# Attention's side products: keys from the query product's free columns, values and output for two groups of heads at once, inverse sums by transfers, diagonal masks off TensorE

## The chip, the cores and the metric

The kernel runs on one core of one Trainium2 chip. The metric is the device time of one execution in microseconds (us). TensorE, VectorE (DVE), ScalarE (ACT), GpSimd (POOL) and SyncE (SP, which here only issues transfers) each work through their instructions in order and wait for each other through semaphores.

## The reference

The input x is 8 sequences of 1024 tokens of 128 features. A layer of relative-position attention with 8 heads of 16 features is followed by a mixture of 8 experts of which each token uses two:

```python
xn = (inputs - mu) / jnp.sqrt(var + 1e-05) * ln_gamma + ln_beta
xh = xn.reshape(b, s, H, Dh)
q = xh @ Wq + bq;  k = xh @ Wk + bk;  v = xh @ Wv + bv
p = pe @ Wp                                   # pe: sine and cosine of the position
content = jnp.einsum('bqhd,bkhd->bhqk', q + u_bias, k)
pos_score = _rel_shift(jnp.einsum('bqhd,khd->bhqk', q + v_bias, p))
attn = softmax((content + pos_score) / sqrt(e))
x = x + jnp.einsum('bhqk,bkhd->bqhd', attn, v).reshape(b, s, e) @ Wo + bo
# then, on layernorm(x): router (two products, layer norm, gelu), softmax, top 2 of 8,
# and for each expert:  x1, x2 = split(h @ W1[e] + b1[e]);  y = (x1 * gelu(x2)) @ W2[e] + b2[e]
output = output + y * expert_mask[:, :, e]    # and x + output
```

The relative shift makes a query's score with keys up to its own position, with the key just after it, and with later keys come from different rows of the position product; the kernel has two tables of key operands for this ("own" and "upper"), and the one key after the query is treated apart, as a band.

## The kernel before, in words

**Tiling.** The eight heads are two groups g of four. Each head has 32 of the 128 partitions: 16 for content and 16 for position. So one score product with 32 rows gives content and position scores together. A block n is a sequence b, a group g and a half qc of the queries (512 of them); there are 32 blocks in the order (b, g, qc). A block has nine units, and the main loop runs over steps t, one unit a step. In each step three blocks' stages overlap:

- side A: scores of queries by keys for the block at t. `greatest` takes each query's row maximum: units "own" (L574, with a table of masks, `wide`), "oth" (the other half of the keys, L570) and one unit "dia" (the four 128x128 blocks on the diagonal). Before the change "dia" adds a mask with a TensorE product (L562) into the bank and reduces it from there (L568).
- side B, 11 steps later: the transposed scores with the shift by the row's maximum (`lower`, L580) and ScalarE's exponential into px (`power`, L587). Upper and lower parts are cut on GpSimd (L597).
- 13 steps later: `weigh`, the product of values and px (av, L631), accumulated over the nine units.

A step has two half-steps, two heads on side A and two on side B in each. Half 0 has the av products, half 1 has `lower`. Each half-step's scores take four of six banks of PSUM; the next half-step's reuse those that the exponentials and the maxima free. A seventh bank, one alone, serves all side products ("ms").

**Side products.** Everything else of attention is written as generators. `aside` is called at the end of each half-step, and takes from the live generators by due time; at most one step that uses the ms bank (`yield 0` asks for it) goes into a half-step, and in half 0 such a step is put off if it is not due. An integer yielded is a number of half-steps to wait. The generators are: `prepare` (layer norm and transpose to xT, once a sequence); `keys` (once per sequence and group: products pq L444 twice for each half of the tokens, multiplied with tables tb on VectorE, L446, and added on GpSimd to z; the content keys' product pk L454; then twelve transfers that place kl and z in shifted copies ku and zu); `values` (product pv L477, transposed to va); `band` (pd, pb L500, pbt L507); `beside` (pm L640 and the band's exponential eb); `close`. After side A's last unit, `shifts` combines the maxima on VectorE (L607 to L613), splits them in three bf16 parts, and TensorE transposes them (mt, L618).

**Closing a block (before).** One column of each head's values is one, so av also holds the sums of the weights. `close` adds av and eb to cx, transposes it to pn (L658), takes the reciprocal of the sums (rd, L660), spreads it on GpSimd (rx, L662), transposes back to pr (L667), multiplies, and projects: po (L673), added to xall (L675).

**Routes and experts.** When the last block of every second sequence is closed, a route is queued: router products, top two, ranks, and 32 indirect transfers a route from GpSimd that scatter the tokens to their experts' rows (xs, L864). These too run beside attention. After attention, 71 blocks of 256 rows pass through the experts (L1189, L1190, L1200), each with its own load of weights (wb).

What stands around the change in the main loop:

```python
if half == 0:
    w = now(t, LAG_W)
    if w:
        weigh(*w)
        if w[1] == NU - 1:
            cl = close(w[0])
            ...
elif ua and ua[1] == NU - 1:
    sh = shifts(ua[0])
    ...
aside(2 * t + half, half == 0)
```

Of the kernel before, what the change touches and what calls it, by code (L numbers as in the profile page):

```python
# [49 lines left out]
P = 128  # L50
NB, S, D = 8, 1024, 128
H, DH = 8, 16
HG = 4
# [19 lines left out]
KB = REG // BT  # L73
# [81 lines left out]
def kernel(ctx: ExitStack, tc: tile.TileContext, a: dict, out: bass.AP):  # L155
# [25 lines left out]
    rows_bc = keep.tile([P, DR + NE], F32, name="rows_bc")  # L181
# [10 lines left out]
    wo_p = [keep.tile([P, D], F32, name=f"wo_p{g}") for g in range(NG)]  # L192
# [4 lines left out]
    rk = ctx.enter_context(tc.tile_pool(name="rk", bufs=1))  # L197
    rk2 = ctx.enter_context(tc.tile_pool(name="rk2", bufs=2))
# [51 lines left out]
    with ExitStack() as at:  # L250
# [34 lines left out]
        wk_p = [acst.tile([P, HG, 32], F32, name=f"wk_p{g}") for g in range(NG)]  # L285
        wv_p = [acst.tile([P, HG, 32], F32, name=f"wv_p{g}") for g in range(NG)]
        wc = [acst.tile([P, 2, P], F32, name=f"wc{g}") for g in range(NG)]
        bias = [acst.tile([P, 4], F32, name=f"bias{g}") for g in range(NG)]

        with tc.tile_pool(name="setup", bufs=1) as sp:  # L290
# [15 lines left out]
            row = sp.tile([1, DR + NE], F32, name="row")  # L306
            nc.scalar.dma_start(row[:, 0:DR], a["br1"].rearrange("(o p) -> o p", o=1))
            nc.scalar.dma_start(row[:, DR:], a["br2"].rearrange("(o p) -> o p", o=1))
            for g in range(NG):
                nc.vector.memset(wo_p[g], 0.0)  # L310
                for j in range(HG):
                    h = HG * g + j
                    nc.scalar.dma_start(wo_p[g][32 * j:32 * j + DH, :], a["Wo"][DH * h:DH * h + DH, :])
                nc.scalar.dma_start(kus[g], a["tab_u"][g])
            nc.scalar.dma_start(wo_p[0][DH:DH + 1, :], a["bo"].rearrange("(o p) -> o p", o=1))
# [21 lines left out]
            nc.tensor.matmul(pb[:, 0:DR + NE], lhsT=ones[0:1, :], rhs=row, start=True, stop=True)  # L337
            nc.vector.tensor_copy(rows_bc, pb[:, 0:DR + NE])
# [9 lines left out]
            wq_p = [sp.tile([P, HG, 32], F32, name=f"wq_p{g}") for g in range(NG)]  # L348
            for g in range(NG):
                for i, t in ((0, wq_p[g]), (1, wk_p[g]), (2, wv_p[g])):  # L350
                    nc.vector.memset(t, 0.0)
                    blocks(t[:, :, 0:DH], i, HG * g, HG)
# [10 lines left out]
            for g in range(NG):  # L363
# [9 lines left out]
                nc.vector.tensor_tensor(wc[g][:, 0, :], wc[g][:, 0, :], wq_p[g].rearrange("p j c -> p (j c)"), ALU.add)  # L373
# [5 lines left out]
                nc.tensor.matmul(pc[:, 2:4], lhsT=ppad, rhs=rp[:, 65:67], start=True, stop=True)  # L379
                nc.vector.tensor_copy(bias[g], pc[:, 0:4])  # L380
                nc.vector.tensor_tensor(bias[g][:, 3:4], bias[g][:, 3:4], cst[:, C_ONE:C_ONE + 1], ALU.add)
# [13 lines left out]
        def prepare(b):  # L395
# [17 lines left out]
            yield  # L413
            xts[b] = xt = ap1.tile([P, S], F32, name=f"xT{b}", tag="xT")
# [8 lines left out]
        def keys(b, g, s):  # L423
# [14 lines left out]
            for hf in range(NQ):  # L438
                c, tb = slice(hf * QB, hf * QB + QB), tbs[hf]
                ts = []  # L440
                for k in range(2):
# [3 lines left out]
                    t = ap1.tile([P, QB], F32, name=f"t{k}{u}_{hf}", tag=f"t{k}")  # L445
                    nc.vector.scalar_tensor_tensor(t, pq, bs[:, k:k + 1], tb[:, k, :], ALU.add, ALU.mult)  # L446
                    ts.append(t)
                    if k == 0:
                        yield
                nc.gpsimd.tensor_tensor(z[:, c], ts[0], ts[1], ALU.add)  # L450
                yield
                yield 0
                pk = bank(f"pk{u}_{hf}")
                nc.tensor.matmul(pk, lhsT=flat(wk_p[g]), rhs=xt[:, c], start=True, stop=True)  # L454
                nc.scalar.activation(kl[:, c], pk, AF.Identity, bias=bs[:, 2:3])
# [11 lines left out]
        def values(b, g, s):  # L467

            u, xt = f"{b}_{g}", xts[b]
            s["vt"] = vt = ap2.tile([P, S + 1], F32, name=f"vt{u}", tag="vt")  # L470
            s["va"] = va = ap2.tile([P, NT, P], F32, name=f"va{u}", tag="va")
            nc.vector.memset(vt[:, S:S + 1], 0.0)
            for hf in range(NQ):
                c = slice(hf * QB, hf * QB + QB)
                yield 0
                pv = bank(f"pv{u}_{hf}")
                nc.tensor.matmul(pv, lhsT=flat(wv_p[g]), rhs=xt[:, c], start=True, stop=True)  # L477
# [861 lines left out]
```

## Time and profile before

| | |
|---|---|
| median of 3 runs | 2161.19 us (2159.23 to 2165.55) |
| profiled execution | 2203.32 us, span 2201.6 us, mean granted TensorE clock 0.952 |
| first scores | at 65.0 us |
| attention | to about 1716 us |
| experts | from about 1724 us |
| TensorE, ScalarE, VectorE, GpSimd busy | 1958.0, 951.4, 1370.8, 742.1 us |
| exponentials px, L587 | 1152 of 594 ns |
| maxima oth, L570, and own, L574 | 512 of 685 ns, 512 of 688 ns |
| maxima dia, L568 | 128 of 686 ns |
| products pq, L444 | 75.0 us in all |

The profile is of one execution, which took longer than the runs that were timed; sums from it are held against its own time. In a line of a group, "x" is the number of instructions and the time behind it the mean of one. A product of 32-bit numbers appears as two instructions. A wait is put down to the instruction that came last, and "issue" is time for which the profile shows no cause. In the chain of what ended last, each row is its start, its length and the work that was waited for.

### The profile page before, as it was taken

To read this page: it belongs to the slowest core of one execution; us is meant where nothing else is said; L and a number is where in the kernel's file an instruction comes from. 1 tells how busy PE (TensorE), PEld (TensorE's weight loads), DVE (VectorE), ACT (ScalarE), POOL (GpSimd) and SP (SyncE) were. 2 spreads that over 40 slices of the span, in tenths; PEclk is the share of its full clock that TensorE was granted. 3 is DMA by queue.
4 is the path that set the end of the run, shared out by engine and by line. 5 is a ranking of instruction groups with operands and counts; after the bars stand their busy time and mean duration, and the time that the engine had idled before them with its cause. 6 is when DMAs were issued, how large, how long until landed. Compare 5 with 4: busy or idle time off the path is not lost.

```text
span 2201.6 us, 40140 instructions
## 1 busy us (share of the span) xinstructions
PE 1958.0 (89%) x15115; PEld 1059.7 (48%) x15115; DVE 1370.8 (62%) x3652; ACT 951.4 (43%) x1767; POOL 742.1 (34%) x895
## 2 busy tenths in 40 slices
PE   4899999999999999889998988998976898799995
PEld 2334444344443444334444433443432687678884
DVE  3476687777777668656876776676651355344454
ACT  0035545455554544445454534454442343234442
POOL 2021223213323331643134254324244244543353
PEclk9999999999999999899999998999996899899998
DMA  5101101101010110201010102010000445455596
GB/s 139 43 14 32 44 1 44 42 4 44 1 44 11 35 36 9 67 17 44 2 44 2 44 28 56 2 44 15 1 18 23 143 156 180 139 173 185 190 304 185
DMA packets 84983, 143.53 MB, mean 65 GB/s; under 512 B 12405, under 2 KB 55558, under 8 KB 84790
## 3 DMA queue, kind: packets, MB, share of 16 engines
q1 hardware_dynamic: 58480, 113.37, 17.8%
q0 software_dynamic: 8912, 18.15, 2.3%
q10 hardware_dynamic: 17398, 9.46, 1.6%
q8 instruction: 119, 1.95, 0.4%
q14 instruction: 74, 0.61, 0.1%
HBM read 105.06 MB, written 23.28 MB: 58 GB/s over the span
## 4 chain that ended last, share of the span: by engine, by line
PE 73%; DVE 11%; POOL 5%; issue 4%; ACT 3%; DMA 2%; another core or an unknown queue 1%; SPq 0%; ACTq 0%; POOLq 0%; DVEq 0%
PE sc L549 27%; PE av L631 10%; PE h L1189 6%; PE h L1190 6%; PE y L1200 5%; DVE jk L574 4%; PE pq L444 3%; PE sc L580 3%; ACT px L587 2%; PE sc L562 2%; PE pb L500 2%; POOL xs L864 2%; PE pk L454 1%; PE pv L477 1%; PE po L673 1%
## 5 line engine op out<-in xcount | busy, mean ns | idle before, releaser
L587 ACT ACTIVATE px<-sc 128x512 f32<-128x512 f32 x1152 | 624.1, 594 | 650.3 <-PE sc L549 310.6
L570 DVE TENSOR_REDUCE oth<-sc 128x1 f32<-128x512 f32 x512 | 330.1, 685 | 209.2 <-PE sc L549 154.9
L549 PE MATMUL sc<-kl,z 32*128 32x512 f32 (+3 forms) x1536 | 411.8, 566 | 44.0 <-ACT px L587 33.1
L574 DVE CUSTOM_DVE_ANT_0 jk<-sc,wide 128x512 f32<-128x512 f32 x512 | 352.2, 688 | 136.4 <-PE sc L549 93.1
L549 PE MATMUL sc<-ku,zu 32*128 32x128 f32 (+3 forms) x2304 | 377.5, 411 | 12.1 <-issue 5.3
L549 PE MATMUL sc<-zu,ku 32*128 32x512 f32 (+3 forms) x1536 | 369.2, 559 | 0.0
L549 PE MATMUL sc<-z,kl 32*128 32x512 f32 (+3 forms) x1536 | 340.9, 525 | 0.0
L631 PE MATMUL av<-px,va 128*32 128x512 f32 (+3 forms) x3072 | 319.3, 512 | 20.7 <-POOL px L597 20.7
L1193 DVE SCALAR_TENSOR_TENSOR gt<-h,wb,gl 128x256 f32<-128x256 f32 x284 | 137.2, 484 | 174.2 <-ACT gl L1192 147.9
L549 PEld LDWEIGHTS sc<-ku,zu 32*128 32x128 f32 x2304 | 196.1, 193 | 64.9 <-ACT px L587 38.5
L549 PEld LDWEIGHTS sc<-kl,z 32*128 32x128 f32 x1536 | 141.3, 191 | 162.8 <-ACT px L587 119.0
L1218 POOL DMA_INDIRECT ys<-yo,to x142 | 137.0, 965 | 236.9 <-DVE to L1214 102.4
L1192 ACT ACTIVATE gl<-h,wb 128x256 f32<-128x256 f32 x284 | 134.0, 473 | 170.7 <-PE h L1190 131.1
L1189 PE MATMUL h<-xt,wb 128*128 128x256 f32 x568 | 177.6, 395 | 32.4 <-ACT yb L1202 15.4
L597 POOL TENSOR_SCALAR_AFFINE_SELECT px<-px 128x516 f32<-128x516 f32 (+1 forms) x128 | 85.7, 669 | 358.2 <-ACT px L587 358.1
L1190 PE MATMUL h<-xt,wb 128*128 128x256 f32 x568 | 174.6, 390 | 0.0
L549 PEld LDWEIGHTS sc<-zu,ku 32*128 32x128 f32 x1536 | 120.7, 191 | 89.7 <-ACT px L587 66.4
L631 PEld LDWEIGHTS av<-px,va 128*32 128x32 f32 x3072 | 70.7, 111 | 187.1 <-issue 118.8
L549 PEld LDWEIGHTS sc<-z,kl 32*128 32x128 f32 x1536 | 129.8, 192 | 61.5 <-ACT px L587 27.7
L580 PE MATMUL sc<-mT,onesb 32*128 32x512 bf16 x1152 | 143.4, 388 | 9.0 <-ACT px L587 9.0
L864 POOL DMA_INDIRECT xs<-rw,slot x128 | 123.9, 968 | 37.3 <-issue 34.0
L1200 PE MATMUL y<-gt,wb 128*128 128x256 f32 x568 | 134.6, 380 | 0.3 <-ACT yb L1202 0.3
(287 smaller groups left out, 2457.1 us busy)
## 6 DMA issues: line engine op xcount, KB each, us to landing
wb<-in_wx SPq DMA_DIRECT2D x71, 772.5 KB
tb<-in_tab SPq DMA_DIRECT2D x32, 768.0 KB
xb<-xs SPq DMA_DIRECT2D x71, 130.0 KB
zu<-z SPq DMA_DIRECT2D x128, 64.0 KB
yk<-ys SPq DMA_DIRECT2D x32, 256.0 KB
ku<-kl SPq DMA_DIRECT2D x64, 64.0 KB
out<-yk ACTq DMA_DIRECT2D x16, 256.0 KB
xall<-in_inputs ACTq DMA_DIRECT2D x7, 512.0 KB
```

The costliest lines, as they stand in the source:

```text
L549: nc.tensor.matmul(ps[:, c0:c0 + w], lhsT=lhs[r, l0:l0 + P], rhs=rhs[r, r0:r0 + w], start=first, stop=final)
L570: nc.vector.tensor_reduce(oth[:, t, j:j + 1], p, AX.X, ALU.max)
L574: nc.vector.tensor_tensor_reduce(jk, p, wide[:, m0:m0 + QB], 1.0, 3.0 * BIG, ALU.add, ALU.max, own[:, t, j:j + 1])
L580: nc.tensor.matmul(p, lhsT=onesb[r, :], rhs=mts[n][r, :], start=first, stop=not first)
L587: nc.scalar.activation(pxs[n, k][:, j, :], p, AF.Exp)
L631: nc.tensor.matmul(avs[n][32 * j:32 * j + 32, c0:c1], lhsT=va[:, kt, 32 * j:32 * j + 32], rhs=px[:, j, c0:c1], start=(k == 0), stop=(k == ...
L864: return nc.gpsimd.indirect_dma_start(xs_v[2 * (t0 + n) + k], bass.IndirectOffsetOnAxis(ap=slot[:, n, k:k + 1], axis=0), rw[:, n, :], None)
L1189: nc.tensor.matmul(ph[:, 1, :], lhsT=wb[:, FF + c * P:FF + (c + 1) * P], rhs=xt, start=True, stop=True)
L1190: nc.tensor.matmul(ph[:, 0, :], lhsT=wb[:, c * P:(c + 1) * P], rhs=xt, start=True, stop=True)
L1193: nc.vector.scalar_tensor_tensor(gt[:, c, :], ph[:, 0, :], wb[:, B1_0 + c:B1_0 + c + 1], gl, ALU.add, ALU.mult)
L1200: nc.tensor.matmul(y, lhsT=wb[:, W2_0 + c * D:W2_0 + (c + 1) * D], rhs=gt[:, c, :], start=(c == 0), stop=(c == NFC - 1))
L1218: ins = nc.gpsimd.indirect_dma_start(ys_v[HB * i + k], bass.IndirectOffsetOnAxis(ap=to[:, k:k + 1], axis=0), yo[:, k, :], None).ins
```

## The change

- Keys: the product of the normalized tokens with `wc[g][:, 1, :]` has 16 columns per head which only position needed. The content keys' weights are added in its other columns, and kl is read from that bank (with a scale of 0 or 1 for each partition) before the product is used up; pk is gone.
- Values: `values` runs once a sequence. Both groups' values are in one product, and va holds for each head group 0's values, a column block of ones, and group 1's values; a group's 32 columns are taken from the middle outward. In group 1 the sums therefore come first. `beside` needs a row of ones in place of the other group's values, which one more GpSimd operation (v1) makes.
- Inverse sums: `close` sends the sums of cx through four transfers to 128 partitions (sm), takes the reciprocal, writes it to memory (inv) and reads it back spread over 16 partitions a head (rx); GpSimd multiplies. The wait between the steps is 3, 3 and 2 half-steps.
- Output: group 0's cx is kept; group 1's is added to it on GpSimd, and one product po with both groups' weights is made for two blocks. The output's bias is added to xall on GpSimd in `prepare`.
- Masks: a "dia" unit's scores are copied to SBUF by ScalarE (up), masked by GpSimd, and reduced by VectorE two half-steps later (`diagonal`).
- Order: `shifts` continues one half-step later. Some buffers change size or share a place, and beside the experts a step that asks for a longer wait gets it.

```diff
         def keys(b, g, s):
...
                     pq = bank(f"pq{u}_{hf}_{k}")
                     nc.tensor.matmul(pq, lhsT=wc[g][:, k, :], rhs=xt[:, c], start=True, stop=True)
-                    t = ap1.tile([P, QB], F32, name=f"t{k}{u}_{hf}", tag=f"t{k}")
+                    t = z[:, c] if k == 0 else ap1.tile([P, QB], F32, name=f"t{u}_{hf}", tag="t")
                     nc.vector.scalar_tensor_tensor(t, pq, bs[:, k:k + 1], tb[:, k, :], ALU.add, ALU.mult)
...
+                nc.scalar.activation(kl[:, c], pq, AF.Identity, bias=bs[:, 2:3], scale=halfs[:, 0:1])
                 nc.gpsimd.tensor_tensor(z[:, c], ts[0], ts[1], ALU.add)
-                yield
-                yield 0
-                pk = bank(f"pk{u}_{hf}")
-                nc.tensor.matmul(pk, lhsT=flat(wk_p[g]), rhs=xt[:, c], start=True, stop=True)
-                nc.scalar.activation(kl[:, c], pk, AF.Identity, bias=bs[:, 2:3])
...
-        def values(b, g, s):
+        def values(b):
...
+                nc.tensor.matmul(pv, lhsT=wv_p.rearrange("p j g d -> p (j g d)"), rhs=xt[:, c], start=True, stop=True)
...
+                to = va[:, hf * TQ:(hf + 1) * TQ].rearrange("p n j o d -> p (n j) o d")
+                pt_ = pt.rearrange("p (m g d) -> p m g d", g=NG, d=DH)
+                for g in range(NG):
+                    nc.scalar.copy(to[:, :, 2 * g, :], pt_[:, :, g, :])
...
         def greatest(n, k, js, ps):
...
+            if kind == "dia":
+                up = ap2.tile([P, len(js), TQ, P], F32, name=f"up{n}_{js[0]}", tag="up")
+                for i, p in enumerate(ps):
+                    nc.scalar.copy(up[:, i].rearrange("p t c -> p (t c)"), p)
+                nc.gpsimd.affine_select(out=up, in_=up, compare_op=ALU.is_ge, fill=BIG, base=-2,
+                                        pattern=[[0, len(js)], [0, TQ], [1, P]], channel_multiplier=-1)
+                return up
...
-                if kind == "dia":
-                    nc.tensor.matmul(p.rearrange("p (t c) -> p t c", c=P), lhsT=identb,
-                                     rhs=mu[:, 0:P].unsqueeze(1).to_broadcast([P, TQ, P]), start=False, stop=True)
...
+        def diagonal(n, js, up):
+
+            nc.vector.tensor_reduce(mx[n][2][:, js[0]:js[0] + len(js), :], up, AX.X, ALU.max)
+            yield
...
         def beside(n):
...
+            v1 = ap1.tile([P, QB], F32, name=f"v1_{n}", tag="pd")
+            nc.gpsimd.tensor_scalar(v1, state[b, g]["vt"][:, q0 + 1:q0 + 1 + QB], halfs[:, g:g + 1], halfs[:, 1 - g:2 - g], ALU.mult, ALU.add)
+            nc.gpsimd.tensor_tensor(eb, eb, v1, ALU.mult)
...
         def close(n):
...
-            yield 0
-            pn = bank(f"pn{n}").rearrange("p (t c) -> p t c", c=P)
...
+            sm = rk2.tile([P, TQ * HG], F32, name=f"sm{n}", tag="sm")
+            for j in range(HG):
+                r = 32 * j + DH * (1 - g)
+                nc.sync.dma_start(sm[32 * j:32 * j + 32, :], cx[r:r + 1, :])
+            yield 3
+            rd = rk2.tile([P, TQ * HG], F32, name=f"rd{n}", tag="rd")
+            nc.vector.reciprocal(rd, sm)
+            nc.sync.dma_start(inv[n % 2], rd)
+            for j in range(HG):
+                r = 32 * j + DH * g
+                nc.sync.dma_start(rxs[g][r:r + DH, :], inv[n % 2][32 * j:32 * j + 32, :].rearrange("(o c) k -> o (c k)", o=1).to_broadcast([DH, QB]))
+            yield 3
+            nc.gpsimd.tensor_tensor(cx, cx, rxs[g], ALU.mult)
+            if g < NG - 1:
+                cxs[b, qc] = cx
+                return
+            nc.gpsimd.tensor_tensor(cx, cx, cxs.pop((b, qc)), ALU.add)
+            yield 2
             yield 0
             po = bank(f"po{n}").rearrange("p (n e) -> p n e", e=D)
             for t in range(TQ):
-                nc.tensor.matmul(po[:, t, :], lhsT=cx[:, t * P:(t + 1) * P], rhs=wo_p[g], start=True, stop=True)
+                nc.tensor.matmul(po[:, t, :], lhsT=cx[:, t * P:(t + 1) * P], rhs=wo_p, start=True, stop=True)
...
                     if ua:
-                        greatest(*ua, ja, pa_)
+                        up = greatest(*ua, ja, pa_)
+                        if up is not None:
+                            live.append(dict(due=t, next=2 * t + half + 2, gap=1, gate=False, steps=diagonal(ua[0], ja, up)))
...
-                        live.append(dict(due=0, next=2 * t + 2, gap=1, gate=False, steps=sh))
+                        live.append(dict(due=0, next=2 * t + 3, gap=1, gate=False, steps=sh))
...
     def beside_experts():
-        if gate[0] > 0 and next(steps, None) == 0:
-            gate[0] = -2
+        if gate[0] > 0:
+            did = next(steps, None)
+            gate[0] = 0 if did is None else -2 if did == 0 else -2 * did
```

## The prediction

> **What bounds the kernel now.** I read the page first: busy shares, then the chain of what ended last, then the chain in order of time for a quiet stretch and for the end of a block, then the waits.
>
> ```profile
> span 2201.6 us, 40140 instructions
> PE 1958.0 (89%) x15115; PEld 1059.7 (48%) x15115; DVE 1370.8 (62%) x3652; ACT 951.4 (43%) x1767; POOL 742.1 (34%) x895
> PE 73%; DVE 11%; POOL 5%; issue 4%; ACT 3%; DMA 2%; another core or an unknown queue 1%; SPq 0%; ACTq 0%; POOLq 0%; DVEq 0%
> ```
>
> TensorE is busy 89% and carries 73% of the chain, so one would say: every TensorE product removed is time. The chain in order of time, inside attention, says where that is not so:
>
> ```profile
> 215.47 1.07 PE sc L549 x8
> 216.54 0.24 PE sc L580 x4
> 216.78 0.59 ACT px L587
> 217.38 0.04 issue
> 217.42 1.14 PE sc L549 x8
> 218.56 1.00 PE av L631 x8
> 219.56 1.07 PE sc L549 x8
> 220.63 0.22 PE sc L580 x4
> 220.84 1.05 PE pb L500 x2
> 221.90 1.07 PE sc L549 x8
> ```
>
> The rows are start, length, what. A step has two half-steps. Half 0 is scores 1.07 and av 1.00: TensorE without a gap, 2.07. Half 1 without a side product is scores 1.07, lower 0.24, and then TensorE waits 0.63 for ScalarE's first exponential, which frees a bank: 1.98. With a 512-wide side product (pb 1.05) it takes 2.34, since the product fills the wait. So a 512-wide product is worth 1.05 in a half 0 but only about 0.35 in a half 1, and a group of four transposes (0.59) in a half 1 is worth nothing.
>
> The other exception is the end of a block:
>
> ```profile
> 246.88 0.60 PE pn L658 x4
> 247.48 0.07 issue
> 247.54 0.69 DVE jk L574
> 248.28 0.64 DVE own L607
> 248.94 0.59 DVE oth L608
> 250.45 0.23 DVE spl L613
> 250.68 0.13 DVE rd L660
> 250.86 0.38 PE mt L618 x4
> ```
>
> Here TensorE stands for VectorE's shift chain. Two totals of waits, with count and longest, name the covers:
>
> ```profile
> POOL px L597 <- ACT px L587: 358.1, 106, 11.5
> PEld sc L549 <- ACT px L587: 251.6, 364, 2.8
> ```
>
> GpSimd mostly waits for work; TensorE's weight loads often wait for ScalarE's exponentials.
>
> **The change part by part.** Times are from the profiled execution, 2203.32 us for a span of 2201.6; it lies 42.1 above the median 2161.19, and I subtract savings from either alike.
>
> *Products removed.* pk 32 x 1.05, pv 16 x 1.05, va's transposes 16 x 0.6, pn and pr 64 x 0.6, po 16 x 1.09, masks (L562, 0.54 a half) 62 x 0.54: about 150 us of TensorE. I sorted the half-steps of the trace by what stands in them, with the measured length of each class, and counted classes before and after from the two orders of instructions:
> - half 0 with a 512-wide product, 3.12 against 2.07 quiet: 60 become 30, 30 x 1.05 = -31.5.
> - half 0 with four transposes, 2.66: 37 become 24, 13 x 0.59 = -7.7.
> - half 1 with a 512-wide product, 2.34: 75 become 70, -1.7.
> - po in half 1, 2.38 against 2.02: 31 become 12, -6.8.
> - half 1 with four transposes, 2.02, quiet 2.02: 83 become 32, nothing. ScalarE's 0.59 exponential hides them; were it gone each would cost 0.59.
>
> Sum -48. So two thirds of the 150 lie where ScalarE sets the pace.
>
> *Masks off TensorE.* A diagonal unit now copies its scores to SBUF on ScalarE (128 copies 128x512, like va's copy 0.590), masks with 64 affine selects on GpSimd (px's at L597 takes 0.67 for 516 elements, so 1.27 by size for 1024), and reduces 64 x 1024 on VectorE two half-steps later. The banks are freed by the copies, behind two exponentials. Half 0: scores 1.08 and three ScalarE operations 1.75 = 2.83; half 1: 1.08 + 0.22 + 1.75 = 3.05. Sum 5.88 a block where the trace has about 5.68 (with its masks): 31 x 0.2 = +6. The masks' 34 us are not gained at all; were the copies free, it would be about -28.
>
> The reduce from SBUF: L568 takes 0.686 for 512, so 1.16 to 1.3. It falls into half-steps that have two reduces already (2 x 0.69 and their gaps, about 1.54 of 2.07), so VectorE gets 0.6 late, twice a block. The next A bank is free only when its first reduce is done; slack there is about 0.25. Bounds 0 (the lag is worked off in the next half-step) and 1.0 a block; where key products' L446 (0.749) comes too I take the lag, else not: 16 x 0.7 = +11.
>
> *Inverse sums by transfers.* pn, rx and pr on TensorE's queue go, and with them the stall at pr for GpSimd's copy: half-steps with pr have mean 2.61, median 2.11, so 27 x 0.5 = -13. VectorE loses the multiply L668 (0.684 x 32) and 16 of the adds L675: beside other work, nothing. Added on SP's queue: four sm transfers, inv and four rx a block, 288 in all. SP's issue takes 0.587 (L463). Behind SP's issue queue are now the twelve key transfers and the next tables: sm waits there up to 12 x 0.59 = 7 us in every other block, and tb (once prefetched right behind the keys) is issued only after the odd block's cx. It has several steps before L446 needs it; nothing, bound +2 a group. The reciprocal waits on VectorE, in order, so a late sm holds both reduces behind it, and TensorE two half-steps on. Three half-steps are 6.2 us; four issues 2.4 and the landing. Here the Trainium skill speaks against the change: "DMA: Bandwidth & Descriptors", "Anatomy of one DMA", gives each transfer a fixed cost of about 2.0 us, most of it completion. With inv and then rx, 2 x 2.0 + 5 x 0.59 = 7 us (an estimate from that page) is past the 6.2 given, and GpSimd's multiply would wait about 1 us a block; the trace shows only that packets of key transfers run 1 to 2 us after issue. By the trace sm is in time and rx is just in time; by the page GpSimd stands 1 us, with 30 of every 48 us idle. Bounds 0 and +30 (VectorE stands 2 us in each of 15 key blocks); I take +5.
>
> *GpSimd's load* grows from about 12 to 17 us a block (64 selects, 32 v1 of 0.6, 48 multiplies and adds of 1.09 to 1.27, less 32 rx of 0.608). It was idle, so nothing by itself. But L607, a VectorE operation with two SBUF inputs, takes 0.174 at least, 0.477 in the median and 2.98 at most in this trace. "SBUF — State Buffer", "Who interferes with whom", says that such an operation is locked out while GpSimd reads SBUF, and a tensor_reduce never is. By the rule the new reduces are safe, but each shift chain can lose a whole select, 32 x 1.27 = +41; by the trace's median, 0.3 more on two operations in a third of the blocks, +7. The trace had many GpSimd operations already: +7.
>
> *Setup and ends.* pk's round trip before the first scores (44.85 to 47.70) goes twice: -6. Ranks of routes end earlier, so the last scatter falls in steady steps, not in the last blocks, where TensorE idles and the clock halves (about 38 us are lost there): bounds -25 and +25, since blocks with scatter take 59 to 61 us, not 45; I take -5. Late steps beside the experts: -2.
>
> Sum: -48 + 6 + 11 - 13 + 5 + 7 - 6 - 5 - 2 = -45. Span 2157, median 2161 - 45 = 2116.
>
> **The rivals.**
> - *TensorE counts in full.* The 73% speaks for it, and that ScalarE is only 43% busy: waits for ScalarE may come out of order of banks, not of its work. Then two thirds of 150, plus the stalls and setup: -80 to -125, 2036 to 2081. Against: the 0.59 hole above recurs in each quiet half 1.
> - *Slower: the diagonal's new path holds VectorE.* In order, copy, select, reduce: copies end 3.4 us after the unit starts, the select 1.3 later, and the reduce comes to VectorE's head at about 8.5. From a GpSimd backlog of 3.8 us at that point on, VectorE waits, its two reduces wait behind it, and TensorE follows. The scatter (L864, 0.968 each at 1.27 pitch, up to three a half-step) makes such a backlog, also for rx and v1; so does a router. It decides where such stalls exceed the 45 us gained: at 4 us each, in 12 blocks. If 16 blocks have one, -45 + 64 = +19, 2180; if eight have one and each chain loses a whole select, -45 + 32 + 34 (41 in place of the 7 above) = +21, 2182; about 2170 to 2196. For: two blocks with scatter already take 59.4 and 61.5. Against: GpSimd has 30 us idle a block.
> - *No difference:* ScalarE's 128 copies (76 us) and VectorE's lag take all that the classes give; 2155 to 2167.
>
> **How the numbers follow.** About 0.3% (6.5 us) is what a measurement of this kernel can tell from no change. The likeliest case has 0.52 and its own range 2085 to 2150; TensorE in full 0.22; no difference 0.07; slower 0.19. The range 2050 to 2188 leaves out about 0.09 at either end. Faster 0.74, same 0.07, slower 0.19.
>
> **What would show it.** Right: quiet half 1 still near 2.0 with px on the chain; the up copies on the chain in two half-steps of about 2.8 and 3.1 a block; pn and pr gone, blocks without router about 43 to 44 us (now 44.1 to 47.1); first scores near 59 instead of 65. Wrong: waits of VectorE's dia reduce for GpSimd, or of rd for the sm transfer, above 20 us in all; L607 above 1 us in the median; blocks with scatter longer than 62. If blocks fall below 42, the first rival holds.

## The result, and the profile after

The changed kernel takes 2143.03 us (median of five runs, 2137.7 to 2146.1) against 2161.44 for the kernel before: ratio 0.9911, 95% interval 0.9892 to 0.9931. That is 18 us faster; 45 were forecast. The time lies in the forecast range, but 27 us of the gain that the sum gave are missing.

One thing has to be known for all that follows: chips differ. On the chip of the timed runs, and on that of one later set, before takes 2160 to 2161 us; on three other chips it takes 2202 to 2209, and the profiled execution of before (2203) has the time of that second kind. Therefore each experiment is given as its ratio to before on its own chip, and compared with the changed kernel's ratio on a chip of the same kind: 0.9929 (interval 0.9914 to 0.9945) on the first kind, called A here, and 0.9982 (0.9969 to 0.9996) on the second kind, B. On B the change gains only 4 us.

The page of the changed kernel (chip of kind A):

```profile
span 2143.6 us, 39397 instructions
PE 1863.5 (87%) x14443; PEld 994.0 (46%) x14443; DVE 1340.2 (63%) x3533; ACT 991.1 (46%) x1879; POOL 907.7 (42%) x1017
```

TensorE lost 94.5 us of busy time, more than five times what the kernel gained. The chain of what ended last breaks off ahead of the experts in this profile, so the waits have to say what stands in attention. First two lines of the waits of before that were not shown, then those of the changed kernel (who waits for whom: us in all, times, longest):

```profile
PEld sc L549 <- DVE own L574: 26.5, 35, 2.4
PEld L618 <- DVE spl L613: 61.2, 30, 4.9
```

```profile
POOL px L620 <- ACT px L610: 352.7, 89, 8.4
PEld sc L565 <- ACT px L610: 308.2, 433, 1.8
PEld sc L565 <- DVE own L592: 84.3, 61, 6.6
ACT kl L466 <- DVE t L462: 62.2, 27, 5.9
PEld sc L565 <- ACT up L579: 33.8, 63, 0.7
DVE z L462 <- DMA tb<-in_tab: 30.2, 14, 4.1
PEld po L701 <- POOL cx L696: 17.7, 8, 2.9
DVE dia L597 <- POOL up L580: 3.8, 1, 3.8
```

The wait for ScalarE's exponential grew from 251.6 to 308.2: where side products were taken away, its hole lies open. The wait for VectorE's own maxima is three times what it was, with single waits of 6.6 us. Sorted by place, though, 54.4 of its 84.3 us lie in unit 0, behind the shift chain, where before the transposes waited 61.2 us for the chain itself (spl): mostly one wait in place of another. Only 13.2 us lie in units 6 and 7. New are the waits for the copies (up), and eight for GpSimd's second operation on cx. The diagonal's reduce waited only once for its select.

To see where in a block time went, I took the start of the first exponential of each half-step from the trace, and averaged the distance to the next by its place in the block (554 half-steps up to the last block; two half-steps a unit). Before (chip B), after (chip A) and after on B (run f2 below), in us a unit:

| unit | 0 | 1 | 2 | 3 | 4 | 5 (dia) | 6 | 7 | 8 | block |
|---|---|---|---|---|---|---|---|---|---|---|
| before | 7.21 | 5.20 | 4.89 | 4.88 | 5.39 | 5.78 | 5.24 | 5.29 | 5.28 | 49.16 |
| after | 7.17 | 5.27 | 4.51 | 4.86 | 5.05 | 5.71 | 6.49 | 5.26 | 4.89 | 49.21 |
| after, f2 | 7.10 | 5.02 | 4.68 | 5.13 | 5.84 | 5.80 | 6.36 | 5.53 | 4.98 | 50.43 |

From the first row to the second, units 2, 4 and 8 won 1.1 us a block, all units but 1 and 6 together 1.27, which is 39 us over 31 blocks. Unit 6, just behind the diagonal, lost 1.25, again 39 us: 17 in the 15 blocks that have key products there, 22 in the 16 others. It loses 1.12 on B too; units 3, 4 and 7 of the third row hold stalls of that chip. In the profiles of the first two rows the steady part of attention is the same to 2 us (1511.8 and 1513.8). The rest of the difference of the two spans is in the last 22 half-steps (79.4 against 39.0) and in what comes after them (488 against 472). The second is chips: on one chip, f1 and f2 below have 487 and 488. The first is not: f1 and f2 have 79 and 36.

The three groups of the masks part, as they came out:

```profile
L580 POOL TENSOR_SCALAR_AFFINE_SELECT up<-up 128x1024 f32<-128x1024 f32 x64 | 70.5, 1104 | 229.8 <-ACT up L579 182.9 <-DVE rs_s L233 23.4 <-DVE z L462 11.8
L597 DVE TENSOR_REDUCE dia<-up 128x8 f32<-128x1024 f32 x64 | 77.7, 1215 | 3.9 <-POOL up L580 3.8
L579 ACT COPY up<-sc 128x512 f32<-128x512 f32 x128 | 69.2, 603 | 8.2 <-PE sc L565 8.2
```

All three are near the durations that were estimated (1.27, 1.16 to 1.3 and 0.590); the select is somewhat shorter. The estimate of the parts was not what failed. Unit 6 of one block, VectorE in the timeline (start, length):

```profile
274.20 0.69 DVE L592 CUSTOM_DVE_ANT_0 jk<-sc,wide 128x512 f32<-128x512 f32 x1 [1.67 <-PE sc L565]
275.03 0.69 DVE L592 CUSTOM_DVE_ANT_0 jk<-sc,wide 128x512 f32<-128x512 f32 x1
275.65 1.21 DVE L597 TENSOR_REDUCE dia<-up 128x8 f32<-128x1024 f32 x1
...
277.82 0.66 DVE L592 CUSTOM_DVE_ANT_0 jk<-sc,wide 128x512 f32<-128x512 f32 x1
...
278.63 0.69 DVE L592 CUSTOM_DVE_ANT_0 jk<-sc,wide 128x512 f32<-128x512 f32 x1
...
279.24 1.22 DVE L597 TENSOR_REDUCE dia<-up 128x8 f32<-128x1024 f32 x1
```

and TensorE in the same stretch:

```profile
276.56 0.40 PE L603 MATMUL sc<-mT,onesb 32*128 32x512 bf16 x4
279.28 1.16 PE L701 MATMUL po<-wo_p,cx 128*128 128x128 f32 x8 [2.32 <-POOL cx L696]
```

VectorE had idled 1.67 us in the diagonal unit. Then two maxima, the late reduce and other work fill it from 274.20 on without a gap, and the next maximum (277.82) comes 0.9 us after TensorE was through with its scores and the lower products (276.96). TensorE itself stands 2.32 us here, for another thing: po waits for GpSimd's addition of the two groups' cx. Both lie in unit 6. Seven of the eight waits of po do, and in them TensorE's products stand 11.2 us.

In a block with key products the late reduce reaches TensorE by another path, over the one bank for side products:

```profile
231.01 1.22 DVE L597 TENSOR_REDUCE dia<-up 128x8 f32<-128x1024 f32 x1
232.15 0.74 DVE L462 SCALAR_TENSOR_TENSOR t<-pq,bias,tb 128x512 f32<-128x512 f32 x1
232.92 0.78 ACT L466 ACTIVATE kl<-pq,bias,halfs 128x512 f32<-128x512 f32 x1 [2.30 <-DVE t L462]
233.75 1.12 PE L460 MATMUL pq<-xT,wc 128*128 128x512 f32 x2 [0.96 <-ACT kl L466]
```

The reduce stands ahead of VectorE's reading of pq, ScalarE's kl waits for that, and TensorE's next product waits for kl. Ten of the fifteen such blocks have this wait, of 0.96 or a little more, in unit 6.

The second place is the shift chain. GpSimd, VectorE and TensorE at the end of the block before a new sequence:

```profile
335.04 1.90 POOL L426 TENSOR_TENSOR xn<-xall,mv 128x1024 f32<-128x1024 f32 x1
337.02 1.93 POOL L427 TENSOR_TENSOR xn<-xn,r 128x1024 f32<-128x1024 f32 x1
338.91 2.33 POOL L429 TENSOR_TENSOR xall<-xall,rows_bc 128x1024 f32<-128x1024 f32 x1
```

```profile
335.52 1.45 DVE L630 TENSOR_TENSOR own<-own,oth 128x16 f32<-128x16 f32 x1
337.00 0.18 DVE L631 TENSOR_TENSOR oth<-bd,dia 128x16 f32<-128x16 f32 x1
337.22 1.76 DVE L632 TENSOR_TENSOR own<-own,oth 128x16 f32<-128x16 f32 x1
339.02 2.29 DVE L633 TENSOR_SCALAR spl<-own 128x16 bf16<-128x16 f32 x1
```

```profile
344.02 1.22 PE L565 MATMUL sc<-kl,z 32*128 32x512 f32 x1 [5.66 <-DVE own L592]
```

Three operations on 16 elements a partition end when a GpSimd operation ends: 335.52 + 1.45 = 336.97 where L426 ends at 336.94, 338.98 where L427 ends at 338.95, 341.31 where L429 ends at 341.24. The chain takes 7.28 us in place of 2.25, TensorE stands 5.66, and its next product takes 1.22, not 0.59; the granted clock there, from 344 to 346 us, is 0.50. L426 and L427 are in the kernel before too (its chain at this place takes 4.38); L429, the bias, is the change's.

### The profile page after: what moved, and what is told of

Same layout as the page of the kernel before. It is cut to its first block, busy times and chain, and to the rows that moved or that the text cites. A ratio compares the mean times of both kernels' runs of the same rounds, so it can differ in the third digit from the quotient of the medians.

```text
span 2143.6 us, 39397 instructions
## 1 busy us (share of the span) xinstructions
PE 1863.5 (87%) x14443; PEld 994.0 (46%) x14443; DVE 1340.2 (63%) x3533; ACT 991.1 (46%) x1879; POOL 907.7 (42%) x1017
## 5 line engine op out<-in xcount | busy, mean ns | idle before, releaser
L565 PE MATMUL sc<-kl,z 32*128 32x512 f32 (+3 forms) x1536 | 442.5, 568 | 101.8 <-DVE own L592 46.7
L565 PE MATMUL sc<-ku,zu 32*128 32x128 f32 (+3 forms) x2304 | 411.0, 422 | 13.4 <-ACT px L610 10.0
L565 PE MATMUL sc<-zu,ku 32*128 32x512 f32 (+3 forms) x1536 | 374.5, 566 | 0.1
L654 PE MATMUL av<-px,va 128*32 128x512 f32 (+3 forms) x3072 | 325.9, 521 | 17.5 <-POOL px L620 15.9
L565 PEld LDWEIGHTS sc<-kl,z 32*128 32x128 f32 x1536 | 149.4, 193 | 239.8 <-ACT px L610 130.3
L565 PEld LDWEIGHTS sc<-ku,zu 32*128 32x128 f32 x2304 | 212.6, 194 | 84.9 <-ACT px L610 51.8
L1219 PE MATMUL h<-xt,wb 128*128 128x256 f32 x568 | 174.0, 389 | 22.6 <-DMA wb<-in_wx 15.7
L1220 PE MATMUL h<-xt,wb 128*128 128x256 f32 x568 | 171.8, 384 | 0.0
L580 POOL TENSOR_SCALAR_AFFINE_SELECT up<-up 128x1024 f32<-128x1024 f32 x64 | 70.5, 1104 | 229.8 <-ACT up L579 182.9
L603 PE MATMUL sc<-mT,onesb 32*128 32x512 bf16 x1152 | 165.1, 385 | 0.0
```

The source lines that it names most:

```text
L565: nc.tensor.matmul(ps[:, c0:c0 + w], lhsT=lhs[r, l0:l0 + P], rhs=rhs[r, r0:r0 + w], start=first, stop=final)
L603: nc.tensor.matmul(p, lhsT=onesb[r, :], rhs=mts[n][r, :], start=first, stop=not first)
L654: nc.tensor.matmul(avs[n][32 * j:32 * j + 32, c0:c1], lhsT=va[:, kt, j].rearrange("p o d -> p (o d)"), rhs=px[:, j, c0:c1], start=(k == 0) ...
L1219: nc.tensor.matmul(ph[:, 1, :], lhsT=wb[:, FF + c * P:FF + (c + 1) * P], rhs=xt, start=True, stop=True)
L1220: nc.tensor.matmul(ph[:, 0, :], lhsT=wb[:, c * P:(c + 1) * P], rhs=xt, start=True, stop=True)
```

## The experiments

**Before and after on other chips (e1, f1; e5, f2).** No edit.

> The kernel before, unchanged, for a second profile. Its first profile was 42 us above the median of its runs, and lost 40 us in its last 22 half-steps. If that tail is the kernel's own, this profile shows the last 22 half-steps at about 79 us again; if it belonged to that one execution, they take about 40 as in the changed kernel and the span is near 2160. In both cases the first 554 half-steps should take about 1512.

> The kernel before again, for a profile on the chip of this set. If this chip is one on which before takes about 2161 us: the profile shows where the 42 us to the other chip lie. Stalls of the tail theory: the last 22 half-steps take about 40 us in place of 75 to 79, the 554 before them 1512 as ever. If instead the loss is spread, each stage is 2% shorter.

> The changed kernel, unchanged, beside the three below on one chip. In the first set of experiments the kernel before took 2202 us, in the run that scored the prediction 2161, so chips differ. If the difference of before and after is the kernels' own, the ratio here is 0.991 again, with the profile's 554 half-steps near 1514 us. If the tail's stalls of 40 us that both profiles of before show belong to the chip on which before takes 2202, and after has none of them there, the ratio is 0.975 to 0.985; in that case after takes about 2160 and the step of the sum that was wrong is not the one of unit 6.

> The changed kernel beside f1, f3 and f4. On a chip with before at 2161 us: 2143, ratio 0.992. On one with before at 2202: not yet measured; tail theory says about 2160 (ratio 0.981), as it has no tail stalls to lose more by.

Before was at 2205.67 and 2200.17 us (ratios 1.0009 and 0.9992, kind B), after at 2142.81 (0.9929, kind A) and 2196.27 (0.9982, kind B). By stages, on B alone, before and after: first exponential at 121.8 and 119.1 us; 554 half-steps in 1509 and 1551; the last 22 in 79 and 36; then 487 and 488. So on B the gain of 43 us in the tail is given back as 42 in the steady part. The changed kernel on A takes 1510 for the same half-steps. Of the 41 us between kinds A and B some 38 are in three places, all beside a scatter of tokens, and 4 in the first half-steps: at the first of the three places two half-steps take 4.9 and 9.3 us on B and 2.3 and 2.1 on A. The theory that the tail's stalls belong to B only and that after is free of them fell: after has such stalls as well, at another place, since its routes run earlier. Kind A gave no profile of before, so how its 18 us are split is not shown.

**Masks back on TensorE (e2, f3).**

```diff
-            if kind == "dia":
-                up = ap2.tile(...)
-                ... nc.scalar.copy(...); nc.gpsimd.affine_select(...)
-                return up
+                if kind == "dia":
+                    nc.tensor.matmul(p..., lhsT=identb, rhs=mu[:, 0:P]..., start=False, stop=True)
...
+                if kind == "dia":
+                    nc.vector.tensor_reduce(dia[:, j, :], p..., AX.X, ALU.max)
```

> The changed kernel with the diagonal masks as TensorE products again (no up copies, no select, no late reduce); all else as changed. Theory A (the late reduce of 1.21 us makes VectorE late in unit 6, and TensorE waits there for a bank, 1.25 us a block): unit 6 goes back from 6.49 to about 5.2 us, 31 blocks, 25 to 40 us faster than the changed kernel, near 2105 to 2118. Theory B (TensorE's products count in full): the 34 us of masks come back, 2165 to 2180. Theory C (ScalarE's copies and the masks just exchange, unit 6 is late for another cause): within 8 us of 2143.

> Masks on TensorE again, beside the changed kernel on one chip. Sum of the separate gains (e8 against e5 was -62): -25 to -40 to the changed kernel, ratio to before 0.974 to 0.981 on a chip with before at 2161.

Measured 0.9782 (0.9751 to 0.9812) and 0.9758 (0.9726 to 0.979) on B, against 0.9982: 44 and 49 us faster than the changed kernel, a little more than theory A's bound (two of e2's six times are 12 to 20 us longer than its other four, f3's lie within 20). Theories B and C fell. The units by f2 and f3: unit 5 5.80 and 5.39, unit 6 6.36 and 5.61, unit 7 5.53 and 5.23. It is not unit 6 alone.

**Masks off TensorE, on the kernel before (g1).** The same part put into before, with the smaller buffers that make room for it.

> The kernel before with one part of the change alone: the diagonal masks off TensorE (copies on ScalarE, select on GpSimd, late reduce on VectorE), and the buffer sizes that the change also has. By the prediction's terms (dia +6, late reduce +11) 17 us slower than before, ratio 1.008. By the undoing on the changed kernel (47 us) up to 1.02. If masks off TensorE only cost in company of the other parts (rival): 0.995 to 1.004.

1.0132 (1.0104 to 1.016), 29 us slower. So the part costs by itself; what the smaller buffers alone cost was not run (f3 has them too). Its units: 5 unchanged (5.75 for 5.78), 6 and 7 slower by 0.55 and 0.5.

**The late reduce (e3, g2, h1).** Three edits of the same thing: two reduces of 512 in four half-steps; the reduce one half-step sooner; the reduce over 16 of 128 columns.

```diff
e3:
+            for i, j in enumerate(js):
+                nc.vector.tensor_reduce(mx[n][2][:, j, :], up[:, i], AX.X, ALU.max)
+                yield
g2:
-    live.append(dict(due=t, next=2 * t + half + 2, ...
+    live.append(dict(due=t, next=2 * t + half + 1, ...
h1:
-            nc.vector.tensor_reduce(..., up, AX.X, ALU.max)
+            nc.vector.tensor_reduce(..., up[:, :, :, 0:16], AX.X, ALU.max)
```

> The changed kernel with the late diagonal reduce of 1024 elements cut into two of 512, one in each of four half-steps of units 6 and 7 in place of one of 1.21 us in each of two. VectorE has 0.17 us more work a block. Theory A (lag of VectorE in unit 6 sets the end): 10 to 30 us faster than 2143, unit 6 at 5.6 or less and unit 7 unchanged. Theory C (something else in unit 6, such as the side product's bank): no change or up to 5 us slower.

> The changed kernel with the diagonal's reduce one half-step after the copies in place of two: half 0's then falls into the second half-step of the diagonal unit, where VectorE has no reduce of its own, and only half 1's into unit 6. Theory A' (the loss is that VectorE stands idle in the diagonal unit and is overfull in unit 6): unit 6 from 6.4 to about 5.7, 12 to 25 us faster than the changed kernel (ratio to before 0.981 to 0.987 where the changed kernel has 0.992; 0.987 to 0.993 where it has 0.998). Rival (ScalarE's copies are what costs): no change.

> The changed kernel with its late diagonal reduce over 16 of the 128 columns (the rest of a row's diagonal is left out of the maximum, which is only the shift of the exponential); copies on ScalarE and select on GpSimd as changed. The reduce falls from 1.21 to about 0.3 us. If VectorE's late reduces are what the masks part costs (theory A): units 6 and 7 go back to the sum that they have with masks on TensorE (10.8 in place of 11.9 us), 25 to 35 us faster than the changed kernel. If ScalarE's copies cost it: 0 to 10 us faster. To the changed kernel that is a ratio of 0.984 to 0.988, or 0.995 to 1.000, whichever chip it is.

All on B, beside 0.9982: e3 0.9948 (0.9925 to 0.997), about 7 us where 10 to 30 were expected; g2 0.9972 (0.9956 to 0.9988), none that can be told; h1 0.9892 (0.9863 to 0.992), 20 us, between what its two theories said. In h1 unit 6 went from 6.36 to 5.86 and unit 7 from 5.53 to 5.37, and the waits of 0.96 for kl became 0.36. In the 15 blocks with key products in unit 6 it went from 6.76 to 5.99, in the other 16 only from 5.99 to 5.74. So VectorE's late reduces make about 20 of the 44 to 49 us. Spreading them moves the lag on (e3: unit 6 5.85, but unit 7 5.86), and with one of them moved into the idle unit (g2) the other still makes the lag: unit 6 falls only to 6.10. Theory A' fell as to its size. The remaining 25 us or so are what is left of the part, ScalarE's copies and GpSimd's selects; no run separates these two. By place, h1 against f3, about 15 lie in the diagonal unit (5.86 and 5.39) and 12 in units 6 and 7. What the waits show is that in h1 TensorE still waits for the copies, and in f3 that entry is gone:

```profile
PEld sc L565 <- ACT up L579: 37.2, 62, 1.7
```

**Preparation earlier (e4, f4; h2 on before).** The whole preparation of a sequence, with GpSimd's long operations, is two steps earlier, away from the chain.

```diff
-                    add(t0 - 3 * NU - 3, t0 - 9, 1, prepare, b)
+                    add(t0 - 3 * NU - 5, t0 - 9, 1, prepare, b)
```

> The changed kernel with the next sequence's preparation started two steps earlier, so that GpSimd's three 1.9 to 2.4 us operations on 128x1024 (two of the layer norm, and the output bias added to xall) no longer run beside VectorE's chain of shifts. Theory A (they lock VectorE's operations on two SBUF inputs out: the chain takes 7.28 us in five of the eight sequences, 2.25 otherwise): the chains go to 2.3 to 4, the gaps of 5.7 us on TensorE ahead of unit 0 vanish, 20 to 30 us faster than 2143. Rival (TensorE would wait there anyway, for the previous reduces): 0 to 8 us.

> Preparation two steps earlier, beside the changed kernel on one chip. By the same sum: -20 to -35 to the changed kernel, ratio 0.976 to 0.983 on a chip with before at 2161.

> The kernel before with only its preparation two steps earlier. In before the chain of shifts takes 4.4 us or more in seven of 32 blocks, beside the layer norm's two GpSimd operations. If that lock costs before as well: 8 to 16 us faster, ratio 0.993 to 0.996. If it was covered there (TensorE had transposes and products of its own to do meanwhile) and only the changed order lays it bare: 0.998 to 1.002.

On the changed kernel 0.9861 and 0.9851 (0.983 to 0.9892, 0.9824 to 0.9877) on B, 27 and 29 us faster. The 32 chains take 81 us in f4 where f2 has 103, and unit 0 went from 7.10 to 6.20. On the kernel before 0.9906 (0.9879 to 0.9932), 21 us, more than expected; its chains went from 93 to 76 (six of them take 4.38 us or more in the trace of before, not seven). The rest of the preparation moves along, but the chains' 22 and 17 us are most of the two gains. So the lock is old: it cost about 21 us before the change, and the change made it dearer.

**The bias alone later (g3).**

```diff
-            nc.gpsimd.tensor_tensor(xall[:, sl, :], xall[:, sl, :], rows_bc...., ALU.add)
             xts[b] = xt = ap1.tile([P, S], F32, name=f"xT{b}", tag="xT")
             for hf in range(NQ):
...
+            nc.gpsimd.tensor_tensor(xall[:, sl, :], xall[:, sl, :], rows_bc...., ALU.add)
```

> The changed kernel with only the added operation of the preparation (output bias onto 128x1024 of xall, 2.4 us on GpSimd) moved behind the transposes of xT. It separates the change's own share of the chain's lock from the layer norm's two operations, which before has as well: chains of 7.28 fall to 4.4, as before has them; 5 to 15 us faster than the changed kernel of the 29 that the earlier preparation gave. If the whole 29 belongs to the added operation: 25 to 30.

0.9938 (0.9916 to 0.996), about 10 us. The chains of 7.4 fall to 5.2 to 5.4, not to the 4.4 expected, and the 10 us is the share of the lock that this operation brought.

**Keys by a product of their own (e6).**

```diff
-                nc.scalar.activation(kl[:, c], pq, AF.Identity, bias=bs[:, 2:3], scale=halfs[:, 0:1])
                 nc.gpsimd.tensor_tensor(z[:, c], ts[0], ts[1], ALU.add)
+                yield
+                yield 0
+                pk = bank(f"pk{u}_{hf}")
+                nc.tensor.matmul(pk, lhsT=wc[g][:, 1, :], rhs=xt[:, c], start=True, stop=True)
+                nc.scalar.activation(kl[:, c], pk, AF.Identity, bias=bs[:, 2:3], scale=halfs[:, 0:1])
```

> The changed kernel with a product of its own for the content keys again, a half-step after the second query product (the same weights, so the same result, and 32 more 128x512 products), and kl read from it. As predicted (free columns save a product: 1.05 in a half 0, 0.35 in a half 1): about 15 to 22 us slower than the changed kernel. Theory A (the bank now has two readers one after the other, VectorE's t and ScalarE's kl, and the next product in the one side bank waits for both: half 1 with pq takes 3.38 in place of 2.35 in 25 half-steps): within 8 us of the changed kernel.

1.0051 (1.0038 to 1.0064) on A beside 0.9929: 26 us slower, more than the 15 to 22 expected. That a saved product gains held, and theory A fell as a sum, though its wait is there in the changed kernel: half-steps 1 with pq take 3.38 us in the median where before has 2.35. About half of them do; the others are at 2.34. With kl out of pq's bank unit 6 is 5.75, the late reduce still in place; units 7 and 8, to which products move, have 5.86 and 6.55.

**Inverse sums by products (e7).** TensorE's two groups of transposes and the multiply on VectorE return, GpSimd spreads the reciprocals as before.

```diff
-            sm = ...; four transfers; yield 3; reciprocal; inv; four transfers to rxs[g]; yield 3
-            nc.gpsimd.tensor_tensor(cx, cx, rxs[g], ALU.mult)
+            ... pn = four transposes of cx; rd = reciprocal(pn); rxs[g] <- rd on GpSimd
+            ... pr_ = four transposes of rxs[g]
+            nc.vector.tensor_tensor(cx, cx, pr_, ALU.mult)
```

> The changed kernel with the inverse sums through TensorE's transposes again (pn, GpSimd's spreading copy, pr, VectorE's multiply), on the new layout of values; output for both groups together as changed. As predicted (transposes in a half 1 are free, in a half 0 they cost 0.59, and pr waits 0.5 for GpSimd; the transfers cost 5): 10 to 20 us slower. Rival (the transfers' waits on VectorE and the late cx cost as much): within 6 us, or faster.

0.9961 (0.9945 to 0.9976) on A: 7 us slower. The transfers help, by less than was expected; the rival's bound of 6 us lies inside the interval.

**Both undone, and a further step (e8, g4).** e8 has masks back and preparation earlier; g4 has masks back too, with preparation four steps earlier, the bias behind the transposes, and `yield 3` ahead of po.

> The changed kernel with both the diagonal masks on TensorE again and the preparation two steps earlier. If the two losses are separate (VectorE late in unit 6; VectorE's shifts beside GpSimd's long operations), their gains add: 35 to 60 us faster than the changed kernel on this chip, a ratio to before of 0.955 to 0.972. If one hides the other, no better than masks back alone, 0.978.

> Masks on TensorE, preparation four steps earlier with the bias behind the transposes, and the output product one half-step later (GpSimd's two operations on cx were what it waited for, 2.3 us at eight blocks). If each takes away a wait of its own: another 10 to 20 us below masks back and preparation earlier (0.963 where before takes 2161), so 0.954 to 0.959. Rival (the waits move on to the next late operation): 0.960 to 0.966.

e8 takes 2080.99 us on A, ratio 0.963 (0.961 to 0.9651): 62 us faster than the changed kernel, just past the 60 expected and somewhat less than the 44 to 49 and 27 to 29 that the two gave one by one on B. It beats both kernels by far. g4 has 0.9649 (0.9623 to 0.9675) on B, where masks back and preparation earlier would add up to 0.963 (f3, f4) or 0.966 (e2, e4); the rival held, and the further edits gave nothing that can be told. No wait of po for cx is left in g4. The page of e8 and the two waits that were read above:

```profile
span 2078.3 us, 39412 instructions
PE 1845.1 (89%) x14571; PEld 986.9 (47%) x14571; DVE 1348.1 (65%) x3597; ACT 929.4 (45%) x1751; POOL 832.2 (40%) x953
```

```profile
PEld sc L565 <- ACT px L608: 350.8, 464, 3.7
PEld sc L565 <- DVE own L590: 48.0, 41, 2.6
```

The wait for VectorE's maxima fell from 84.3 to 48.0 and its longest from 6.6 to 2.6: in unit 0, by the earlier preparation, from 54.4 to 31.6, and in units 6 and 7, by the masks, from 13.2 to 3.1. The bound is again ScalarE's exponential.

## Why the prediction was right or wrong

*The masks part, +6 and +11 together +17: the step that failed.* On kind B it measures 44 to 49 us in company of the other parts (e2, f3), and 29 alone (g1). The sum without it was -62; with masks back the kernel takes 48 to 53 us less than before. So 27 to 32 us of the miss of 41 on B belong to this part, and 9 to 14 to all others. On A, the kind of the timed runs, it was undone only together with the preparation (e8, 62 us). Its two terms:

*The diagonal unit, 5.88 a block: right in size (5.71), wrong as a comparison.* It was held against 5.68 of before (5.78 in the table). But without the masks part this unit too would have lost its side products: f3 has 5.39. The part thus takes 0.4 a block, 13 us, where the sum charged 6.

*The late reduce, 16 x 0.7 = +11: mis-sized.* h1 measures this term at 20 us. In the key blocks the lag was what I took: 0.77 in each of 15, 12 us. What I set at nothing is the rest: 0.25 in the other 16 blocks of unit 6 and 0.16 in unit 7, 9 us. The path was not the one forecast either: in the key blocks TensorE waits not for the next A bank but for the side bank, whose second reader kl stands behind VectorE's late reading of pq. The part's total on VectorE even fell, from 82.4 to 77.7 us: it was moved from a unit where VectorE has nothing else to do into one where it is full. The two terms make about 33 of the 44 to 49; how the other 12 or so in units 6 and 7 come about stays open.

*Classes of half-steps, -48, and the stall at pr, -13: somewhat too much.* No run separates them; with the rest of the sum they came out at 48 to 53 of 62 (B). Two subtractions were missed. pq's bank now has two readers in turn (ScalarE's kl waits for VectorE's t, 62.2 us in all), and po waits for GpSimd's second operation (11.2 us of TensorE in unit 6); I had put that work down as hidden because GpSimd is idle on average. The three terms of a quiet half 1 add up to 1.94, not 1.98; nothing hangs on it.

*The clock: not in the sum.* Over the 554 half-steps TensorE's granted clock is 0.965 and 0.967 before (before, f1), and 0.953, 0.958 and 0.947 after (after, e5, f2). If all that is missing to 1 is time at half clock, that is about 100 us before and 126 to 164 after (an estimate from these figures); at most half of the difference, 13 to 32 us, can be lost time. No run separates it. It is not how the masks part costs: f3 has 0.948.

*GpSimd's lock on the chain, +7: near, for the chain.* The chains' sum went from 93 to 103 us. What carried it was not the select, whose bound was 41, but one added operation of 2.4 us that runs beside the chain in five sequences; moved away, it gives 10. The rule of the Trainium skill ("SBUF — State Buffer", "Who interferes with whom") was the better guide to the place than the median row was: I had looked at L607's median and not at which GpSimd operations stand beside its largest values. They cost before about 21 us that I had not seen at all.

*Inverse sums, +5: within.* VectorE waited 14.5 us in all for sm. GpSimd waited 26.3 for rx, of which 20.2 is one wait; the other five are 6.1 together. The 2.0 us that I took from the Trainium skill ("DMA: Bandwidth & Descriptors", "Anatomy of one DMA") stand there for transfers that GpSimd issues, and these are issued by SyncE; rx took 1.8 us from issue to landing in the median. The wait of 1 us a block that I worked out did not come. e7 values the whole part, with the stall at pr, at 7 us.

*The tables' load, costed at nothing:* VectorE waited 30.2 us for it in 14 waits, the whole of the bound. Unit 4, where it falls, still won 0.34 on A.

*Setup -6:* 3 (122.1 to 119.1). *Tail -5:* it depends on the chip; on B the tail gained 43 and the steady part gave 42 back. "I subtract savings from either alike" was wrong: the same change is worth 18 us on one chip and 4 on another.

*The rivals.* TensorE in full is refuted. Slower through a reduce that waits for its select did not happen: that wait is 3.8 us in all. 2143 lies within the range of the likeliest case (2085 to 2150), but not for its reason. In what it says, the third, with the smallest chance, came nearest: on B the masks part, ScalarE's copies and VectorE's lag in it, took nearly all that the rest gave. Of the signs named, the first scores came at 61.3 us (59 forecast, 65 before), and the early blocks did not settle at 43 to 44: blocks 2 to 5, counted from 0, take 41.4, 44.7, 45.0 and 45.4 us where before has 44.4, 44.1, 44.8 and 44.0.

## What to carry to other kernels

Work that leaves a busy engine is worth what its half-step loses, and must be charged where it arrives: sort the trace by the place in the loop, and ask of each moved operation how full the receiving engine is in that very stretch, not on average. Compare a moved part with what its place would be with all the other parts done, not with the place before. And look at which long operations run beside a short chain that everybody waits for: here moving a sequence's preparation, with its three GpSimd operations, by two steps was worth 27 to 29 us on chips on which the whole change was worth 4.

## What the runs showed of the hardware

A 16-element VectorE operation with two SBUF inputs waited for the end of a GpSimd operation on 128x1024 (1.45 us for 0.46 in the median of its line, and 1.76 for 0.18), as the page cited above says; L633, with one SBUF input, waited too (2.29 us for 0.20), which I had not expected.

The chips of kind B lose time beside the scatter: the same program, at its first scatter and the load of tables, first on B (f2), then on A (e5). Columns after the stretch and its length: busy time of TensorE, weight loads, VectorE, ScalarE, GpSimd, the granted clock, the share of DMA, GB/s.

```profile
801.80:806.80 5.00, 2.69 (x13) 0.91 (x10) 0.85 (x2) 1.19 (x2) 3.78 (x5) 0.80 0.96 315
806.80:811.80 5.00, 1.67 (x2) 0.09 (x1) 0.00 (x0) 0.00 (x0) 2.57 (x3) 0.50 0.50 131
```

```profile
796.00:801.00 5.00, 5.00 (x52) 2.15 (x48) 1.95 (x4) 2.83 (x6) 3.78 (x5) 1.00 0.79 232
801.00:806.00 5.00, 4.55 (x46) 2.37 (x42) 1.62 (x4) 3.45 (x8) 4.07 (x5) 1.00 0.69 197
```

On B VectorE and ScalarE do nothing for five microseconds while GpSimd's transfers go on, and TensorE's clock is halved. ScalarE's next exponential then has this entry in the timeline:

```profile
812.46 1.09 ACT L610 ACTIVATE px<-sc 128x512 f32<-128x512 f32 x2 [6.66 <-remote]
```

The profile does not name the releaser. What holds the engines, and why only on some chips, stays open.
